# Counting sparse-graph edges by pairs of nodes: shared slots for every pair, and 512 instead of 496 counted chunks

## The chip, the cores and the metric

The kernel runs on one core of one Trainium2 chip. The time is the device time of one launch in microseconds (us), the median of several executions. The engines named below are PE (TensorE: matmuls), PEld (its weight loads), DVE (VectorE), ACT (ScalarE), POOL (GpSimd, which issues the indirect gathers) and SP (SyncE, which issues the plain transfers).

## The reference

A graph layer: 12,500 nodes with 128 features, 200,000 edges sorted by destination, four edge types. The destinations are drawn as 12500 times the square of a uniform number, so that nodes with low numbers have very many edges (several hundred for the first ones) and nodes with high numbers have some eight.

```python
h = jnp.maximum(_layernorm(x, axis=-1), 0.0)
xs = h[src]
msgs = 0
for i in range(4):
    msgs = msgs + where(edge_type == i, xs @ W[i] + b[i], 0.0)
out = x + segment_sum(msgs, dst, num_segments=12500)
```

## The kernel before

Edges are cut into 1563 chunks of 128. The first C0 = 496 chunks (the edges of the low-numbered, crowded nodes) are **counted**; the other TM = 1067 chunks are **gathered**.

**Gathered chunks.** They go in groups of G = 16. For each chunk POOL issues one indirect DMA that fetches the 128 source rows (`gather`, line 450, issue at line 456). The first RAW = 8 groups fetch rows of x and normalize them on the way (the raw stage), because the table of normalized rows, `htab`, is being built in that time; later groups fetch rows of `htab`, each in three bf16 parts. `sum_up` (line 469) makes one-hot matrices on DVE (line 479), multiplies rows by them on PE (line 517; three matmuls for a chunk), copies the sums to SBUF on ACT (line 524), multiplies by W on PE (line 534) and adds the result into a ring of nodes on DVE (line 546). The gathered rows lie in five buffers of eight chunks, so POOL can be up to forty chunks ahead of PE.

**Counted chunks.** For a counted node nothing is gathered. The kernel makes the matrix "how many edges of type t come from source node s" and multiplies the whole table by it. Sources are split into a block number (NW = 98 blocks) and a place in it (128). `make_slots` (line 676) sorts the edges of the counted nodes into **slots**, columns of 128 edges that belong to one node or to a pair, and leaves for each slot two vectors: `loT` (place of the source) and `hkT` (block and type of the source, 1 to 392). It runs within the raw stage, a few steps in each group (SLOT_STEPS, line 68), and what is left at the end of group 7. `levels[k]` is how many nodes (or pairs) are given a (k+1)-th slot.

`count` (line 808) turns slots into counts: DVE makes two one-hot matrices for a slot, `o1` (128 edges by 128 places, lines 820 and 824) and `o2` (128 edges by 392, line 825); PE multiplies them (line 829) into a PSUM tile of 128 by 392; slots of the same **unit** are summed there; ACT writes the result as 16-bit integers and reads the sum out (line 832). A unit holds two nodes: edges of the first weigh 1, edges of the second 256, so that the two bytes of an integer are the counts of the two nodes, and are later read as two 8-bit floats. Below node PAIRS = 558 a node has slots of its own, and a unit sums up to two slots of the one node with weight 1 and up to two of the other with weight 256 (a fixed number in the instruction). From node 558 up two neighbours share one slot, and each edge has its own weight in `byT` (a second per-edge vector in the instruction, line 823).

`multiply` (line 853) takes a **batch** of up to VBMAX = 112 nodes (56 units): it streams the whole table from DRAM and multiplies each block's three parts by the counts (line 864): 98 x 3 = 294 matmuls with 112 x 4 = 448 columns each. One such round over the table is called a pass. Then come eight small matmuls by W (line 879) and additions into `acc`, the sums of the counted nodes (line 887).

**Order.** `dense_work` (line 909) runs the count of a batch beside the multiply of the batch before; the first batch is counted with no multiply beside it. `pace` (line 896) spreads this work evenly, by columns, over the gathered groups from group 8 to the last full one; what is left goes in there, and the last small groups (12, 8, 4 and 3 chunks) follow. With 496 chunks the planner's lines 103 to 166 give: ND = 1304 counted nodes, NS = 1496 slots made, NSLOTS = 1123 slots counted (neighbours share from 558 on) in 670 units, in 12 batches: one of 108 nodes, 11 of 112. The batches have 54, 137, 137, 112, 83 (seven times) and 102 slots. The gathered chunks make 65 full groups and the four small ones.

Of the kernel before, what the change touches and what calls it, by code (L numbers as in the profile page):

```python
# [48 lines left out]
P = 128  # L49
# [7 lines left out]
C0 = 496  # L57
VBMAX = 112
MANY = 16
HB = 4  # L60
# [11 lines left out]
def kernel(  # L72
# [31 lines left out]
    ND = int(N * q**2 + 5 * 2 * q * N * (q * (1 - q) / E) ** 0.5) // 8 * 8 + 8  # L104
    caps = []
    for d in range(ND):
        many = E * (((d + 1) / N) ** 0.5 - (d / N) ** 0.5)
        caps.append(max(1, -(-int(many + 6 * many**0.5) // P)))
# [8 lines left out]
    def window_of(c):  # L117
# [8 lines left out]
    PAIRS = next(  # L126
        d
        for d in range(levels[1] + levels[1] % 2, ND, 2)
        if (lambda m: m + 6 * m**0.5)(E * (((d + 2) / N) ** 0.5 - (d / N) ** 0.5)) <= P
    )  # L130
    alone = [(k, d) for k in range(0, len(levels), 2) for d in range(min(levels[k], PAIRS))]
    if len(alone) % 2:
        alone.append(None)
    shared = [(0, d) for d in range(PAIRS, ND)]

    VB = VBMAX
    left = len(alone) + len(shared)
    sizes_of = ([left % VB] if left % VB else []) + [VB] * (left // VB)
    batches = []
    a = b0 = 0  # L140
    for i, n in enumerate(sizes_of):

        na, ns = len(alone) - a, len(shared) - b0
        n1 = 0 if i < 1 else min(round(n * na / (na + ns) / 2) * 2, na)
        n1 = max(n1, n - ns)
        batches.append(alone[a : a + n1] + shared[b0 : b0 + n - n1])
        a, b0 = a + n1, b0 + n - n1
    assert a == len(alone) and b0 == len(shared)

    def slots_of(u):  # L150

        if u[0] is not None and u[0][0] == 0 and u[0][1] >= PAIRS:
            return [(u[0][1], None)]
        got = []
        for v, by in zip(u, (1.0, 256.0)):
            if v is not None:
                k, d = v
                got.append((starts_of[k] + d, by))
                if k + 1 < len(levels) and d < levels[k + 1]:
                    got.append((starts_of[k + 1] + d, by))  # L160
        return got

    def units(vs):
        return [tuple(vs[i : i + 2]) for i in range(0, len(vs), 2)]

    NSLOTS = sum(len(slots_of(u)) for vs in batches for u in units(vs))
# [138 lines left out]
    def prep_dense():  # L305
# [7 lines left out]
        nc.vector.tensor_single_scalar(first1, di[:, n, 0], 1.0, op=ALU.add)  # L313
# [4 lines left out]
        nc.vector.tensor_scalar(what[:, 0], di[:, n], 1.0, 2047.0, ALU.add, ALU.min)  # L318
# [8 lines left out]
        nc.vector.tensor_sub(what[:, 1], lo[:, n], over[:, n])  # L327
# [10 lines left out]
    nc.vector.tensor_copy(iota_b, iota_i)  # L338
    iota_f = prep.tile([P, P], F32, name="iota_f")
# [336 lines left out]
    def make_slots(dix):  # L676
# [4 lines left out]
        nth = dix.tile([P, ND], F16, name="nth")  # L681
        packed = dix.tile([P, NS], I32, name="packed")
        cnt12 = dix.tile([N3, NS], BF16, name="cnt12")
        for a in range(0, ND, NB):
            z = min(a + NB, ND)
            nc.vector.tensor_single_scalar(d1[:, a:z], iota_n[:, : z - a], float(a), op=ALU.add)
# [20 lines left out]
        yield from pipelined(first_chunk(a, z) for a, z in pieces(ND))  # L707
        d = 0
        while d < ND:
            e = d  # L710
            while e < ND and caps[e] == caps[d]:
                e += 1
            nc.vector.tensor_scalar(nth[:, d:e], d1[:, d:e], 0.0, float(caps[d]), ALU.mult, ALU.add)
            d = e
        nc.vector.tensor_add(nth, nth, qa[:, :ND])
# [6 lines left out]
        def pick_out(q, a, z, before):  # L722
# [20 lines left out]
            if before:  # L743
                nc.vector.tensor_mul(mask[:, :n], pv[:, :n], mask[:, :n])
                nc.vector.tensor_add(packed[:, a:z], packed[:, a:z], mask[:, :n])
            else:
                nc.vector.tensor_mul(packed[:, a:z], pv[:, :n], mask[:, :n])

        jobs = []
        for a, z in pieces(NS):  # L750
            jobs.append(pick_out(qa, a, z, False))
            if a < ND:
                jobs.append(pick_out(nth, a, min(z, ND), True))
        yield from pipelined(jobs)

        def unpack(a, z):
            n = z - a
            hk = dix.tile([P, 512], I32, name="hk")
            nc.vector.tensor_single_scalar(hk[:, :n], packed[:, a:z], 7, op=ALU.arith_shift_right)
            nc.vector.tensor_copy(hkT[:, a:z], hk[:, :n])  # L760
            nc.vector.scalar_tensor_tensor(
                loT[:, a:z], hkT[:, a:z], float(-P), packed[:, a:z], op0=ALU.mult, op1=ALU.add
            )

            nc.vector.tensor_single_scalar(hk[:, :n], hk[:, :n], NT - 1, op=ALU.bitwise_and)
            ohs = []
            for t in range(NT):
                is_t = dix.tile([P, 512], BF16, name="sel", bufs=2 * DENSE)
                if t < NT - 1:
                    nc.vector.tensor_single_scalar(is_t[:, :n], hk[:, :n], t + 1.0, op=ALU.is_equal)  # L770
                else:
                    nc.vector.tensor_single_scalar(is_t[:, :n], hkT[:, a:z], 0.5, op=ALU.is_gt)
                ohs.append(is_t)
            yield True
            pn = x_ps.tile([N3, 512], F32, name="pt")
            for t in range(NT):
                nc.tensor.matmul(pn[:, :n], pick_a[:, t, :], ohs[t][:, :n], start=(t == 0), stop=(t == NT - 1))
            nc.scalar.copy(cnt12[:, a:z], pn[:, :n])
# [4 lines left out]

        one, two = slice(PAIRS, ND, 2), slice(PAIRS + 1, ND, 2)
        nc.vector.tensor_scalar(byT, hkT[:, two], 0.5, 255.0, ALU.is_gt, ALU.mult)
        nc.vector.tensor_single_scalar(byT, byT, 1.0, op=ALU.add)
        for of in (loT, hkT):
            nc.vector.tensor_tensor(of[:, one], of[:, one], of[:, two], ALU.add)
        nc.vector.memset(seen, 0.0)
        nc.vector.tensor_reduce(seen[:N3], cnt12, AX.X, ALU.add)  # L790

        for a, z in pieces(ND):
            pn = x_ps.tile([P, 512], F32, name="pt")
            todo = [k for k, n in enumerate(levels) if n > a]
            for k in todo:
                n = min(levels[k], z) - a
                nc.tensor.matmul(
                    pn[:, :n],
                    b12,
                    cnt12[:, starts_of[k] + a : starts_of[k] + a + n],  # L800
                    start=(k == todo[0]),
                    stop=(k == todo[-1]),
                )
            yield True
            nc.vector.tensor_tensor(acc[:, a:z], acc[:, a:z], pn[:, : z - a], ALU.add)


    def count(vs, counts):
        todo = []
        for i, u in enumerate(units(vs)):  # L810
            of = slots_of(u)
            todo += [(i, c, by, n == 0, n == len(of) - 1) for n, (c, by) in enumerate(of)]
        both = sdp.tile([P, VB // 2], F32, name="both", bufs=2)
        for s0 in range(0, len(todo), OB):
# [3 lines left out]
            for k, (i, s, by, first, last) in enumerate(part):  # L818
                if by == 1.0:
                    nc.vector.tensor_scalar(o1[:, k, :], iota_b, loT[:, s : s + 1], None, ALU.is_equal)  # L820
                else:
                    if by is None:
                        by = byT[:, (s - PAIRS) // 2 : (s - PAIRS) // 2 + 1]
                    nc.vector.tensor_scalar(o1[:, k, :], iota_b, loT[:, s : s + 1], by, ALU.is_equal, ALU.mult)  # L824
                nc.vector.tensor_scalar(o2[:, k, :], iota_n, hkT[:, s : s + 1], None, ALU.is_equal)  # L825
            for k, (i, s, by, first, last) in enumerate(part):
# [12 lines left out]
        n = len(vs) // 2  # L839
# [13 lines left out]
    def multiply(vs, counts):  # L853
        nv = len(vs)
# [26 lines left out]
        while i < nv:  # L881
            if vs[i] is None:
                i += 1
                continue
            k, d = vs[i]
            n = next((m for m in range(1, nv - i) if vs[i + m] != (k, d + m)), nv - i)
            nc.vector.tensor_tensor(acc[:, d : d + n], acc[:, d : d + n], py[:, i : i + n], ALU.add)
            i += n
# [17 lines left out]
    def dense_columns():  # L906
        return NSLOTS * float(NB) + sum(len(vs) for vs in batches) * NW * 3.0 * NT

    def dense_work():
# [5 lines left out]
        total = dense_columns() + sum(len(slots_of(u)) for u in units(batches[0])) * (alone_slot - a_slot)  # L915
        gone = 0.0
        before = None
        for vs in batches + [None]:
            steps = {}
            now = None  # L920
            if vs:
                now = vs, dense.tile([P, NW, VB // 2 * NT], U16, name="counts")
                steps[count(*now)] = sum(len(slots_of(u)) for u in units(vs)) * (a_slot if before else alone_slot)
            if before:
                steps[multiply(*before)] = len(before[0]) * a_node
# [21 lines left out]
    byT = slots.tile([P, (ND - PAIRS) // 2], F32, name="byT")  # L947
# [268 lines left out]
```

## Time and profile before

| | |
|---|---|
| median of 12 runs | 1398.63 us (1395.96 to 1399.77) |
| the profiled execution's own time, and its span | 1400.13 us, 1398.4 us |
| mean granted TensorE clock | 0.951 |
| busy: PE, DVE, ACT, POOL | 1277.6, 990.1, 600.5, 1041.8 us |
| multiply matmuls (line 864) | 3528, 736.2 us |
| count matmuls (line 829) | 1123, 271.5 us |
| gathers (line 456) | 128 of x, 939 of the table; 128.9 and 911.3 us |
| evictions of counts (line 832) | 670, mean 504 ns, and 670 reads of the sum, mean 211 ns |

The profile is of one execution. Busy times of an engine are sums of its instructions' times without double counting within the engine; a group's mean duration includes pipelining, so that the distance between starts of two neighbours is often shorter than the mean. A line of the table of groups reads: source line, engine, operation, output and inputs, shapes, number, busy time and mean, and then how long the engine had been idle before these instructions and what ended that.

### The profile page before, as it was taken

To read this page: it belongs to the slowest core of one execution; us is meant where nothing else is said; L and a number is where in the kernel's file an instruction comes from. 1 tells how busy PE (TensorE), PEld (TensorE's weight loads), DVE (VectorE), ACT (ScalarE), POOL (GpSimd) and SP (SyncE) were. 2 spreads that over 40 slices of the span, in tenths; PEclk is the share of its full clock that TensorE was granted. 3 is DMA by queue.
4 is the path that set the end of the run, shared out by engine and by line. 5 is a ranking of instruction groups with operands and counts; after the bars stand their busy time and mean duration, and the time that the engine had idled before them with its cause. 6 is when DMAs were issued, how large, how long until landed. Compare 5 with 4: busy or idle time off the path is not lost.

```text
span 1398.4 us, 28832 instructions
## 1 busy us (share of the span) xinstructions
PE 1277.6 (91%) x8981; PEld 764.3 (55%) x8981; DVE 990.1 (71%) x5329; ACT 600.5 (43%) x1993; POOL 1041.8 (74%) x1077
## 2 busy tenths in 40 slices
PE   1655887899999999999989999999999999999995
PEld 1434554455655555565545555555555555555563
DVE  8778897888888767675756675768766767775334
ACT  6766746335325245353443443534434335334111
POOL 7777757777777777777777777777777777777774
PEclk9985667899999999999999999999999999999997
DMA  6552333565665666666657666666666666666663
GB/s 166 188 153 95 137 108 88 149 189 181 200 181 174 196 192 201 193 203 192 206 156 209 185 205 193 192 198 197 195 194 191 194 194 189 187 188 186 212 193 97
DMA packets 129448, 249.81 MB, mean 179 GB/s; under 512 B 25255, under 2 KB 72025, under 8 KB 129289
## 3 DMA queue, kind: packets, MB, share of 16 engines
q1 hardware_dynamic: 80121, 147.17, 33.9%
q0 software_dynamic: 49168, 100.76, 24.9%
q8 instruction: 71, 1.16, 0.3%
q14 instruction: 88, 0.72, 0.1%
HBM read 231.80 MB, written 16.03 MB: 177 GB/s over the span
## 4 chain that ended last, share of the span: by engine, by line
PE 80%; DVE 11%; ACT 5%; issue 2%; DMA 0%; POOL 0%; DVEq 0%; SPq 0%; ACTq 0%
PE pa L864 46%; PE pt L829 13%; PE py L534 9%; PE ps L517 8%; ACT h L408 2%; DVE st L389 2%; ACT counts L832 2%; DVE ring L546 2%; PE ps L502 1%; DVE h L428 1%; PE py L879 1%; DVE oh L479 1%; DVE ohf L479 1%; DVE o L824 1%; PE pt L576 1%
## 5 line engine op out<-in xcount | busy, mean ns | idle before, releaser
L456 POOL DMA_INDIRECT hm<-htab,srcT x939 | 911.3, 971 | 300.0 <-issue 262.8
L864 PE MATMUL pa<-counts,hs 128*128 128x448 fp8e4 (+1 forms) x3528 | 736.2, 353 | 1.0 <-ACT counts L832 0.9
L864 PEld LDWEIGHTS <-hs 128*128 128x128 bf16 x3528 | 343.6, 98 | 306.9 <-issue 15.0
L832 ACT ACTIVATE counts<-pt 128x392 uint16<-128x392 f32 x670 | 328.1, 504 | 254.4 <-PE pt L829 251.9
L825 DVE TENSOR_SCALAR o<-iota_n,hkT 128x392 bf16<-128x392 f16 x1123 | 374.7, 334 | 0.0
L829 PE MATMUL pt<-o,o 128*128 128x392 bf16 x1123 | 271.5, 334 | 5.3 <-ACT counts L832 3.1
L546 DVE TENSOR_TENSOR ring<-ring,py 128x20 f32 (+7 forms) x1040 | 177.9, 171 | 92.7 <-PE py L534 70.3
L524 ACT COPY sb<-ps 128x224 f32<-128x224 f32 (+8 forms) x267 | 103.1, 394 | 255.8 <-PE ps L517 220.2
L479 DVE TENSOR_SCALAR oh<-iota_b,keyT 128x56 bf16<-128x56 bf16 (+7 forms) x939 | 163.3, 262 | 57.1 <-PE ps L517 55.5
L820 DVE TENSOR_SCALAR o<-iota_b,loT 128x128 bf16<-128x128 bf16 x375 | 100.0, 267 | 113.2 <-PE pt L829 106.1
L824 DVE TENSOR_SCALAR o<-iota_b,loT,byT 128x128 bf16<-128x128 bf16 x373 | 126.2, 338 | 58.2 <-PE pt L829 55.5
L456 POOL DMA_INDIRECT hm<-in_x_dram,srcT x128 | 128.9, 1007 | 40.7 <-issue 36.0
L534 PE MATMUL py<-sb,wsb 128*128 128x224 f32 (+7 forms) x520 | 146.7, 427 | 0.7 <-ACT sb L524 0.5
L517 PEld LDWEIGHTS <-hm 128*128 128x128 bf16 x2817 | 122.0, 99 | 45.2 <-DMA hm<-htab,srcT 6.7
L517 PE MATMUL ps<-oh,hm 128*128 128x56 bf16 (+7 forms) x2817 | 137.3, 198 | 5.3 <-DMA hm<-htab,srcT 5.0
L832 ACT ACTIVATION_READ_ACCUMULATOR counts<-pt 128x1 f32 x670 | 141.1, 211 | 0.0
L829 PEld LDWEIGHTS <-o 128*128 128x128 bf16 x1123 | 101.4, 99 | 71.7 <-DVE o L825 7.7
L534 PEld LDWEIGHTS py<-sb,wsb 128*128 128x128 f32 x520 | 101.3, 211 | 31.9 <-issue 7.5
L506 ACT CAST cnt<-ps 128x320 bf16<-128x320 f32 (+9 forms) x69 | 26.5, 384 | 207.3 <-PE ps L502 189.8
L517 PE MATMUL ps<-ohf,hm 128*128 128x40 f32 (+1 forms) x256 | 60.7, 400 | 58.7 <-ACT hm L408 58.6
L824 DVE TENSOR_SCALAR o<-iota_b,loT 128x128 bf16<-128x128 bf16 x375 | 98.2, 262 | 8.7 <-PE pt L829 8.5
L517 PEld LDWEIGHTS ps<-ohf,hm 128*128 128x128 f32 x256 | 54.7, 308 | 75.3 <-ACT hm L408 62.2
(188 smaller groups left out, 625.6 us busy)
## 6 DMA issues: line engine op xcount, KB each, us to landing
hs<-htab SPq DMA_DIRECT2D x288, 384.0 KB
hm<-htab,srcT POOLq DMA_INDIRECT x939
htab<-h SPq DMA_DIRECT2D x11, 768.0 KB
xo<-in_x_dram SPq DMA_DIRECT2D x23, 256.0 KB
out_dram<-xo SPq DMA_DIRECT2D x23, 256.0 KB
xt<-in_x_dram SPq DMA_DIRECT2D x6, 512.0 KB
hs<-htab SPq DMA_DIRECT2D x12, 192.0 KB
xt<-in_x_dram SPq DMA_DIRECT2D x5, 448.0 KB
```

The lines of the kernel that those rows point to most:

```text
L456: nc.gpsimd.indirect_dma_start(out=rows[:, (i - h0) * width : (i - h0 + 1) * width], out_offset=None, in_=table, in_offset=bass.IndirectOf ...
L479: nc.vector.tensor_scalar(oh[:, i, :], (iota_f if raw else iota_b)[:, :K], keyf[:, (t0 + i) % (TURN * P) : (t0 + i) % (TURN * P) + 1], Non ...
L517: mm = nc.tensor.matmul(ps[:, i - i0, :], rows(i, c, nparts), oh[:, i, :], start=(c == 0), stop=(c == nparts - 1),)
L524: nc.scalar.copy(sb[:, i0:i1].rearrange("p g t n -> p g (t n)"), ps[:, : i1 - i0, :])
L534: mm = nc.tensor.matmul(py[:, :g, :], wsb[:, t, :], sb[:, :g, t, :], start=False, stop=(t == NT - 1))
L546: nc.vector.tensor_tensor(to, to, py[:, i, :], ALU.add)
L820: nc.vector.tensor_scalar(o1[:, k, :], iota_b, loT[:, s : s + 1], None, ALU.is_equal)
L824: nc.vector.tensor_scalar(o1[:, k, :], iota_b, loT[:, s : s + 1], by, ALU.is_equal, ALU.mult)
L825: nc.vector.tensor_scalar(o2[:, k, :], iota_n, hkT[:, s : s + 1], None, ALU.is_equal)
L829: nc.tensor.matmul(pb, o1[:, k, :], o2[:, k, :], start=first, stop=last)
L832: nc.scalar.activation(counts[:, :, i * NT : (i + 1) * NT], pb.rearrange("p (b t) -> p b t", t=NT), AF.Copy, accum_out=both[:, i : i + 1],)
L864: nc.tensor.matmul(pa[:, : nv * NT], hs[:, j - j0, c * D : (c + 1) * D], counts[:, j, : nv * NT], start=(j == 0 and c == 0), stop=(j == NW ...
```

## The change

Two things are changed together.

First, the form of the slots. All counted nodes are taken as pairs of neighbours (2u, 2u+1); U = ND / 2 pairs. The edges of a pair share slots from the first one on, each edge carries its weight (1 or 256) in `byT`, and a unit is one pair, which sums up to SL = 4 slots. A pair with more than four slots has several units. `o1` is now always made with two per-edge vectors. To keep the parity of the destination, its bit is carried in the packed number (doubled place of the source, plus the bit), so `prep_dense` has more operations, and `unpack` takes the bit out, makes `byT` for all slots and counts edges by type twice (all edges, and those of odd nodes). `iota_2` holds even numbers to compare with the doubled places.

Second, C0 goes from 496 to 512: 512 chunks are counted and 1051 are gathered. With it the same planner lines give ND = 1392, NS = NSLOTS = 1080 slots in 711 units, in 13 batches: one of 39 units (78 nodes) and 12 of 56 (112 nodes); 39, 124, 104, 83 and then 79 or 80 slots for each, 93 in the last. The gathered chunks make 64 full groups and the same four small ones.

```diff
-C0 = 496
+C0 = 512
+SL = 4
...
+    U = ND // 2
     caps = []
-    for d in range(ND):
-        many = E * (((d + 1) / N) ** 0.5 - (d / N) ** 0.5)
+    for u in range(U):
+        many = E * (((2 * u + 2) / N) ** 0.5 - (2 * u / N) ** 0.5)
         caps.append(max(1, -(-int(many + 6 * many**0.5) // P)))
...
+    both_of = [(k, u) for k in range(0, len(levels), SL) for u in range(levels[k])]
+    double = [(k, u) for k, u in both_of if k + 1 < len(levels) and u < levels[k + 1]]
+    single = [v for v in both_of if v not in double]
     VB = VBMAX
-    left = len(alone) + len(shared)
+    left = len(both_of)
-    sizes_of = ([left % VB] if left % VB else []) + [VB] * (left // VB)
+    sizes_of = ([left % (VB // 2)] if left % (VB // 2) else []) + [VB // 2] * (left // (VB // 2))
...
+    def slots_of(v):
+        k, u = v
+        return [starts_of[m] + u for m in range(k, min(k + SL, len(levels))) if u < levels[m]]
...
+        nc.vector.tensor_single_scalar(pair[:, n], di[:, n], 1, op=ALU.arith_shift_right)
+        nc.vector.tensor_single_scalar(first1, pair[:, n, 0], 1.0, op=ALU.add)
...
+        nc.vector.tensor_single_scalar(di[:, n], di[:, n], 1, op=ALU.bitwise_and)
...
+        nc.vector.tensor_sub(bo[:, n], lo[:, n], over[:, n])
+        nc.vector.scalar_tensor_tensor(what[:, 1], di[:, n], 0.5, bo[:, n], op0=ALU.mult, op1=ALU.add)
...
+            nc.vector.tensor_single_scalar(par[:, :n], packed[:, a:z], 1, op=ALU.bitwise_and)
...
+            nc.vector.tensor_sub(loT[:, a:z], loT[:, a:z], par[:, :n])
+            nc.vector.tensor_scalar(byT[:, a:z], par[:, :n], 255.0, 1.0, ALU.mult, ALU.add)
...
+            for second in (False, True):
+                if second:
+                    nc.vector.scalar_tensor_tensor(
+                        hk[:, :n], par[:, :n], float(NT), hk[:, :n], op0=ALU.mult, op1=ALU.add
+                    )
...
+        nc.vector.tensor_sub(cnt12, cnt12, cnt2)
...
-            for k, (i, s, by, first, last) in enumerate(part):
-                if by == 1.0:
-                    nc.vector.tensor_scalar(o1[:, k, :], iota_b, loT[:, s : s + 1], None, ALU.is_equal)
-                else:
-                    if by is None:
-                        by = byT[:, (s - PAIRS) // 2 : (s - PAIRS) // 2 + 1]
-                    nc.vector.tensor_scalar(o1[:, k, :], iota_b, loT[:, s : s + 1], by, ALU.is_equal, ALU.mult)
+            for k, (i, s, first, last) in enumerate(part):
+                nc.vector.tensor_scalar(
+                    o1[:, k, :], iota_2, loT[:, s : s + 1], byT[:, s : s + 1], ALU.is_equal, ALU.mult
+                )
...
     def multiply(vs, counts):
-        nv = len(vs)
+        nv = 2 * len(vs)
```

## The prediction

> **What bounds the kernel now.** First the page's busy shares and slices, to see where each engine is full.
>
> ```profile
> PE 1277.6 (91%) x8981; PEld 764.3 (55%) x8981; DVE 990.1 (71%) x5329; ACT 600.5 (43%) x1993; POOL 1041.8 (74%) x1077
> ...
> PE   1655887899999999999989999999999999999995
> ...
> DVE  8778897888888767675756675768766767775334
> ...
> POOL 7777757777777777777777777777777777777774
> PEclk9985667899999999999999999999999999999997
> ```
>
> PE is full from the eighth slice on. POOL is level at seven tenths from beginning to end, which looks like slack and is not, as its timeline shows:
>
> ```profile
> 1379.70 0.95 POOL L456 DMA_INDIRECT hm<-htab,srcT  x1 [0.31 <-issue]
> 1380.95 0.95 POOL L456 DMA_INDIRECT hm<-htab,srcT  x1 [0.30 <-issue]
> 1382.21 0.95 POOL L456 DMA_INDIRECT hm<-htab,srcT  x1 [0.30 <-issue]
> ```
>
> A gather starts every 1.254 us, and the idle 0.30 us is "issue", no wait for a buffer. This spacing holds all through: 1067 x 1.254 = 1338 us, the last at 1382. So two engines are near their limits: POOL needs 16 x 1.254 = 20.07 us for a group, and PE must fit a group's share of counted work into the same time. Whether PE does is read from the busy times in five stages (raw groups, their second half, the first batch's count alone, the main stage, the tail); columns: length, PE, PEld, DVE, ACT, POOL, granted clock, DMA share, GB/s.
>
> ```profile
> 0.00:120.00 120.00, 57.77 (x212) 42.29 (x213) 98.35 (x547) 81.54 (x195) 90.24 (x100) 0.91 0.55 165
> 120.00:217.00 97.00, 73.79 (x319) 48.32 (x318) 81.02 (x386) 55.57 (x140) 64.60 (x62) 0.66 0.33 110
> 217.00:252.00 35.00, 26.64 (x164) 13.33 (x163) 29.44 (x149) 28.89 (x117) 26.46 (x29) 0.74 0.27 77
> 252.00:1357.00 1105.00, 1092.79 (x8060) 641.58 (x8059) 762.95 (x4154) 427.51 (x1526) 840.54 (x868) 0.99 0.64 191
> 1357.00:1399.00 42.00, 26.62 (x233) 18.80 (x232) 18.37 (x98) 7.03 (x16) 19.91 (x21) 0.83 0.44 125
> ```
>
> The main stage leaves PE 1105 - 1092.8 = 12.2 us idle, at clock 0.99. A busy PE need not be at its peak, so the last view is the PE timeline inside it:
>
> ```profile
> 696.08 2.43 PE L864 MATMUL pa<-counts,hs 128*128 128x448 fp8e4 x12
> 698.35 0.66 PE L829 MATMUL pt<-o,o 128*128 128x392 bf16 x3
> 698.85 0.42 PE L517 MATMUL ps<-oh,hm 128*128 128x64 bf16 x9
> ...
> 699.60 2.43 PE L864 MATMUL pa<-counts,hs 128*128 128x448 fp8e4 x12
> 701.87 0.66 PE L829 MATMUL pt<-o,o 128*128 128x392 bf16 x3
> 702.37 2.43 PE L864 MATMUL pa<-counts,hs 128*128 128x448 fp8e4 x12
> 704.64 0.27 PE L532 MATMUL py<-cnt,b 128*128 128x256 bf16 x1
> ```
>
> By distances of starts, 12 multiply matmuls take 698.35 - 696.08 = 2.27 us, 0.189 us each, and three of a count 0.50, 0.166 each. 448 / 0.189 and 392 / 0.166 are both 2.37 columns a ns: time goes with columns, back to back. In the main stage every column added on PE is time added.
>
> **The passes.** Before: 11 passes of 448 columns and one of 432. After: 12 of 448 and one of 78 x 4 = 312. With 0.189 us for 448, by columns 0.182 for 432 and 0.132 for 312, the difference is 294 x (0.189 + 0.132 - 0.182) = **+40.9 us**. If the short matmuls took as long as the full ones it would be 294 x 0.196 = +57.6; two rows lie on one line through zero, so I take columns. The lower end is 294 x (0.189 + 0.098 - 0.182) = +31, with 0.098 us for a weight load of the same line if columns cost less than that. The eight small matmuls by W of a pass took 0.9 us (726.06 to 726.95): **+0.9**.
>
> Here a rule can be weighed. The Trainium skill's "TensorE: Matmul & The Clock Gate", section "Back-to-back issue gap", gives N / 2.4 + 2.5 ns for isolated matmuls, but says that in a stream of weight loads and matmuls N = 512 sustains some 131 ns. For 448 columns the first is 189.2 ns, which the timeline agrees with; the second, scaled to 448 columns (115 ns), would make the extra pass cost an estimated 25 us, and the trace, a stream of just that kind, does not show it.
>
> **The slots in the main stage.** Before, 1123 - 54 = 1069 slots; after, 1080 - 39 = 1041. On PE -28 x 0.166 = **-4.6 us**.
>
> **The gathered group.** 16 chunks fewer: one group of window 12 less on PE (the raw stage keeps eight groups). 48 matmuls at 0.04 us (12 in about 0.5), 0.3 for its counts by type, 0.1 for the bias, and the multiply by W: 256 columns took 706.48 - 704.75 = 1.73 us, so 192 take 1.3. Sum **-3.7 us**. POOL loses 16 x 1.254 = 20.1 us; as PE is full, this is no gain by itself.
>
> **The first batch alone.** In 217 to 252 PE waits 0.15 us after each count, for ACT or DVE:
>
> ```profile
> 244.70 0.33 PE L829 MATMUL pt<-o,o 128*128 128x392 bf16 x1 [0.15 <-ACT counts L832]
> 245.18 0.33 PE L829 MATMUL pt<-o,o 128*128 128x392 bf16 x1 [0.15 <-ACT counts L832]
> 245.66 0.33 PE L829 MATMUL pt<-o,o 128*128 128x392 bf16 x1 [0.15 <-ACT counts L832]
> ```
>
> A slot costs 0.48 us here, so 15 fewer are -7.2 us; if the whole stage scales, 35 x 15 / 54 = -9.7; if only PE's own time counted, -5. I take **-7.2**, the measured distance. The pacing puts 54 x 2.5 x 392 extra columns into its total before and 39 x 2.5 x 392 after, so about 2.0 groups lie in this stage before and 1.4 after; 0.6 of a group moves to the main stage: **+2.3**.
>
> **The slot making, in the raw stage.** On PE the selecting matmuls lose 608 + 1024 columns times 4 and 8 or so, the counting by type gains: in all some 12,000 columns fewer, at the 1.1 to 1.9 columns a ns that these ran at (clock 0.66) about -8 us. On DVE first-chunk search and selecting save about 8 us, but `unpack` has 14 operations on a piece instead of seven (each 0.41 to 0.67 us for 512): 3 x 3.6 = 10.4 us become 2.1 x 7.3 = 15.4; with the removed pair additions (-2), the new subtraction, more levels and `prep_dense`, DVE comes out within 1 us of before. The order shifts: more steps (25 instead of 23, by my count of the generator's yields) are left over for the end of group 7, where nothing hides them. ACT, DVE and PE take turns on the chain in this stage, so PE's saving counts in part: **-3**, ends -8 (all of it) and +5 (the longer `unpack` alone on the path).
>
> **The second batch.** Its count (124 slots) runs beside the short pass. DVE needs 0.22 + 0.23 us for a slot with two vectors (start to start; 0.16 + 0.23 without): 124 x 0.45 = 56, plus 3.8 groups at some 5.3 us and 4 us of small work, 80 us. PE has 38.8 + 124 x 0.166 + 3.8 groups x 4.7 = 77. So DVE ends last by a little, and whatever waits for `o2` in PE's order waits too: **+3**, ends 0 (DVE was at 82.05 of 95 us beside 137 slots in before's third batch, and PE had no gap) and +12 (gaps as at 700 to 740, where DVE, PE and gathers waited for each other, 5.7 us idle and the clock down to 0.86). In other batches DVE needs 80 x 0.45 + 4.5 x 5.3 + 4 = 64 of about 91 us: hidden by PE. ACT has 41 evictions more, about 0.47 us start to start, hidden by its idle half.
>
> **What no longer waits.** A group will need 20.5 us of PE against POOL's 20.07, so gathers stay ahead and the waits at 700 to 740 should shrink: **-4**, ends 0 and -8. In the tail PE is idle for 42 - 26.6 = 15.4 us, some of it behind the last gathers, which end about 20 us earlier against a dense end that comes later: **-2**, ends 0 and -8. The rest of the tail is the ring additions and output, unchanged.
>
> **Sum.** 40.9 + 0.9 - 4.6 - 3.7 - 7.2 + 2.3 - 3 + 3 - 4 - 2 = **+22.6 us** on the profiled execution's 1400.13. That execution is 1.5 us above the median, so I predict 1398.6 + 22.6 = 1421 us.
>
> **Rivals.** *Gathers bound it.* If the pass finds room on PE and POOL sets the end, 16 gathers fewer give 1398.6 - 20.1 = 1379. For it: POOL's unbroken spacing to 1382. Against it: PE would need 41 us of idle time in the main stage and has 12.2. It decides from the point where PE work for a group falls under 20.07 us; I find 20.5. *The savings are at their far ends*: -9.7, -8, -8, -8, no cost in the second batch: about +5, 1404. For it: raw stage and tail have PE idle in plenty. Against: they would all have to come. *DVE becomes the bound.* All 1080 `o1` take the 338 ns form, some 0.06 us longer by starts than the 750 that had a fixed weight or none. With bursts of DVE work in the batches of 124 and 104 slots and PE's clock falling with each gap, +10 to +25 more, about 1440. Against: average use stays near 70%. *It doesn't do what it says* (fewer than 13 batches, or the check of the slots failing): the sizes follow from constants, 711 / 56 = 12.7.
>
> **How the numbers follow.** About 0.2% (2.8 us) is what a measurement of this kernel tells from no change. Forecast (1410 to 1432) 0.72; DVE rival (1432 to 1450) 0.12; savings at their ends (1400 to 1410) 0.10, a fifth of it within 0.2%; gathers bound 0.05; the rest 0.01. Leaving out the gathers' case, the lower part of the savings' and the upper of DVE's, the range is 1405 to 1435, and the likeliest case's own is 1410 to 1432. Faster 0.05, same 0.03, slower 0.92.
>
> **What would show it.** Multiply matmuls 3822, about 189 ns apart; 711 evictions; 1051 gathers; the first count alone some 7 us shorter; PE full between it and the last pass, and POOL now waiting for PE's buffers (a gap other than 0.30 us) before the end. Wrong would be: PE idle of over 20 us in the main stage (DVE), an end that follows the last gather by 15 us as now (gathers bound), or the raw stage ending more than 8 us off 217.

## The result, and the profile after

| | before | after |
|---|---|---|
| median | 1398.57 us (28 runs, 1395.96 to 1400.39) | 1418.7 us (7 runs, 1417.4 to 1423.58) |
| ratio, 95% interval | | 1.0154 [1.0145, 1.0164] |
| profiled execution: own time, span | 1400.13, 1398.4 us | 1417.24, 1415.4 us |

The kernel is slower by 20.1 us by the medians; 1421 had been forecast. The runs of after lie in two clumps, four at 1417.4 to 1418.7 and three at 1422.1 to 1423.6, for a reason that was not found, and the profiled execution is in the lower one, so that the two traces differ by 17.0 us only; what is said below of stages is set against those 17.0.

Busy shares and slices, from the page of after:

```profile
PE 1299.3 (92%) x9205; PEld 785.9 (56%) x9205; DVE 1005.6 (71%) x5244; ACT 620.2 (44%) x2074; POOL 1021.4 (72%) x1061
...
PE   1647888889999999999999999999999999999995
...
DVE  8787888887876776766767667687677666776324
...
POOL 7777667777767777777777777776777767777762
PEclk9986557999999999999999999999999999999999
```

PE has 21.7 us more to do, POOL 20.4 us less. POOL's last slice fell from 4 to 2: the last gather is issued 24.2 us ahead of the end, instead of 16.2. How the gathers are issued is seen in POOL's timeline and its waits of after:

```profile
670.30 0.95 POOL L450 DMA_INDIRECT hm<-htab,srcT  x1 [0.31 <-issue]
...
674.43 0.97 POOL L450 DMA_INDIRECT hm<-htab,srcT  x1 [3.19 <-PE pt L835]
...
1391.20 0.95 POOL L450 DMA_INDIRECT hm<-htab,srcT  x1 [0.30 <-issue]
```

```profile
POOL hm L450 <- PE pt L835: 45.7, 49, 3.2
POOL hm L450 <- PE ps L511: 9.8, 10, 3.1
```

(A line of waits reads: who waits, for whom; us in all, times, longest.) These are 59 waits for PE, 55.5 us together. 25 of them are no longer than the steady 0.30 us of issue, and before has such ones too; the other 34 last 0.4 to 3.2 us, 47.8 us together, and before has none of these: POOL is so far ahead that no buffer is free. This is the turn of the bound that was forecast. 1051 gathers need 1318 us at 1.254 us; PE no longer lets them go at that speed.

For the readings by stage I cut both traces at the same four events: the first count alone, the first multiply matmul, the end of the first pass, and the end of the last pass. Columns as before: length, PE, PEld, DVE, ACT, POOL, clock, DMA share, GB/s. First the kernel before, cut in this new way, then after:

```profile
0.00:216.73 216.73, 131.29 (x528) 90.49 (x529) 179.10 (x930) 137.09 (x334) 154.57 (x161) 0.80 0.46 141
216.73:252.31 35.58, 27.21 (x170) 13.70 (x168) 29.79 (x151) 28.90 (x118) 27.04 (x29) 0.74 0.28 79
252.31:350.20 97.89, 93.78 (x724) 54.90 (x723) 82.56 (x456) 35.71 (x132) 74.72 (x77) 0.95 0.60 180
350.20:1356.10 1005.90, 997.80 (x7337) 585.88 (x7333) 679.90 (x3697) 391.26 (x1396) 764.76 (x792) 1.00 0.64 192
1356.10:1399.00 42.90, 27.52 (x239) 19.35 (x236) 18.79 (x98) 7.57 (x17) 20.66 (x22) 0.83 0.44 124
```

```profile
0.00:217.26 217.26, 131.71 (x554) 92.11 (x555) 178.44 (x955) 138.11 (x337) 158.88 (x165) 0.78 0.46 142
217.26:241.56 24.30, 18.73 (x147) 9.47 (x144) 22.85 (x123) 21.25 (x89) 18.69 (x19) 0.74 0.28 79
241.56:323.30 81.74, 73.21 (x601) 50.45 (x602) 72.18 (x354) 32.56 (x124) 62.36 (x64) 0.94 0.67 201
323.30:1376.80 1053.50, 1051.30 (x7674) 615.76 (x7673) 714.01 (x3718) 420.68 (x1513) 769.78 (x803) 1.00 0.65 194
1376.80:1416.00 39.20, 24.39 (x238) 18.08 (x236) 18.14 (x97) 7.58 (x17) 11.69 (x13) 0.93 0.39 112
```

| stage | before | after | difference |
|---|---|---|---|
| raw groups and slot making | 216.7 | 217.3 | +0.5 |
| first count alone | 35.6 | 24.3 | -11.3 |
| first pass, beside the second batch's count | 97.9 | 81.7 | -16.2 |
| the other passes | 1005.9 | 1053.5 | +47.6 |
| tail, to the span's end | 42.3 | 38.6 | -3.7 |

The main stage (rows three and four) grew by 31.4 us: PE's busy time by 32.9, its idle time from 12.2 to 10.7. So it is work on PE, not waiting, that made the kernel slower. Inside, the idle time has moved: beside the first pass it rose from 4.1 to 8.5, in the rest it fell from 8.1 to 2.2, with PE busy 99.8% of 1053 us. Waits for gathered rows are gone from PE's matmuls on them, as their lines on the pages of before and after show (the last numbers are PE's idle time just ahead of them):

```profile
L517 PE MATMUL ps<-oh,hm 128*128 128x56 bf16 (+7 forms) x2817 | 137.3, 198 | 5.3 <-DMA hm<-htab,srcT 5.0
```

```profile
L511 PE MATMUL ps<-oh,hm 128*128 128x56 bf16 (+7 forms) x2769 | 136.2, 198 | 0.0
```

That a short pass is priced by its columns is seen in PE's timeline of after:

```profile
241.56 1.75 PE L870 MATMUL pa<-counts,hs 128*128 128x312 fp8e4 x12
243.15 0.33 PE L835 MATMUL pt<-o,o 128*128 128x392 bf16 x1
```

12 matmuls of 312 columns take 1.59 us from start to start, 0.1325 us each; 0.132 had been forecast from the 448-column ones. The figure for isolated matmuls in the Trainium skill ("TensorE: Matmul & The Clock Gate", section "Back-to-back issue gap") puts 312 columns at an estimated 132.5 ns, and the timeline agrees.

### The profile page after: what moved, and what is told of

Same layout as the page of the kernel before. It is cut to its first block, busy times and chain, and to the rows that moved or that the text cites. A ratio compares the mean times of both kernels' runs of the same rounds, so it can differ in the third digit from the quotient of the medians.

```text
span 1415.4 us, 29284 instructions
## 1 busy us (share of the span) xinstructions
PE 1299.3 (92%) x9205; PEld 785.9 (56%) x9205; DVE 1005.6 (71%) x5244; ACT 620.2 (44%) x2074; POOL 1021.4 (72%) x1061
## 3 DMA queue, kind: packets, MB, share of 16 engines
q1 hardware_dynamic: 83659, 156.80, 35.3%
q0 software_dynamic: 48400, 99.19, 24.7%
## 4 chain that ended last, share of the span: by engine, by line
PE 80%; DVE 12%; ACT 4%; issue 2%; DMA 1%; DVEq 1%; SPq 0%; ACTq 0%
PE pa L870 48%; PE pt L835 12%; PE ps L511 8%; PE py L528 8%; DVE st L383 2%; ACT h L402 2%; DVE ring L540 2%; DVE oh L473 1%; PE ps L496 1%; PE py L885 1%; DVE o L828 1%; DVE ohf L473 1%; DVE h L422 1%; ACT counts L838 1%; DVE o L831 1%
## 5 line engine op out<-in xcount | busy, mean ns | idle before, releaser
L450 POOL DMA_INDIRECT hm<-htab,srcT x923 | 889.9, 964 | 329.4 <-issue 265.6
L870 PE MATMUL pa<-counts,hs 128*128 128x448 fp8e4 (+1 forms) x3822 | 779.6, 349 | 0.7 <-issue 0.5
L870 PEld LDWEIGHTS <-hs 128*128 128x128 bf16 x3822 | 372.8, 98 | 323.1 <-issue 10.6
L828 DVE TENSOR_SCALAR o<-iota,loT,byT 128x128 bf16<-128x128 bf16 x1080 | 361.7, 335 | 193.2 <-PE pt L835 187.1
L838 ACT ACTIVATE counts<-pt 128x392 uint16<-128x392 f32 x711 | 348.0, 504 | 210.9 <-PE pt L835 209.7
L831 DVE TENSOR_SCALAR o<-iota_n,hkT 128x392 bf16<-128x392 f16 x1080 | 353.2, 327 | 0.0
L518 ACT COPY sb<-ps 128x192 f32<-128x192 f32 (+8 forms) x263 | 101.9, 392 | 295.5 <-PE ps L511 279.3
L473 DVE TENSOR_SCALAR oh<-iota_b,keyT 128x56 bf16<-128x56 bf16 (+7 forms) x923 | 159.9, 260 | 62.6 <-PE ps L511 62.3
L500 ACT CAST cnt<-ps 128x224 bf16<-128x224 f32 (+10 forms) x68 | 26.2, 385 | 210.9 <-PE ps L496 189.2
L511 PE MATMUL ps<-ohf,hm 128*128 128x40 f32 (+1 forms) x256 | 64.1, 413 | 55.1 <-ACT hm L402 55.1
L402 ACT ACTIVATE hm<-hm,nmr,rstd 128x128 f32<-128x128 f32 x128 | 51.0, 481 | 8.8 <-DVE nmr L393 8.3
L402 ACT ACTIVATE h<-xt,nmrt,rstdt 128x128 f32<-128x128 f32 x98 | 39.3, 483 | 0.0
```

The lines of the kernel that those rows point to most:

```text
L402: nc.scalar.activation(h(k), xt(k), AF.Relu, bias=nmr[:r, k : k + 1], scale=rstd[:r, k : k + 1])
L450: nc.gpsimd.indirect_dma_start(out=rows[:, (i - h0) * width : (i - h0 + 1) * width], out_offset=None, in_=table, in_offset=bass.IndirectOf ...
L473: nc.vector.tensor_scalar(oh[:, i, :], (iota_f if raw else iota_b)[:, :K], keyf[:, (t0 + i) % (TURN * P) : (t0 + i) % (TURN * P) + 1], Non ...
L511: mm = nc.tensor.matmul(ps[:, i - i0, :], rows(i, c, nparts), oh[:, i, :], start=(c == 0), stop=(c == nparts - 1),)
L518: nc.scalar.copy(sb[:, i0:i1].rearrange("p g t n -> p g (t n)"), ps[:, : i1 - i0, :])
L828: nc.vector.tensor_scalar(o1[:, k, :], iota_2, loT[:, s : s + 1], byT[:, s : s + 1], ALU.is_equal, ALU.mult)
```

## The experiments

Two theories stood against each other at first. Mine: PE is full, the 13th pass is paid in full, and the new slots are a gain that is too small to pay for it. The rivals: gathers set the end, or DVE (all `o1` with two vectors, batches of 124 and 104 slots) does.

### e1: the new slots with the old 496 chunks

```diff
-C0 = 512
+C0 = 496
```

> The new slots with 496 counted chunks, so that only the form of the slots differs from before (1036 slots instead of 1123, 667 units instead of 670, still 12 passes; 51, 128, 107, then 82 slots in a batch). PE theory with a gather floor: PE loses (1069 - 985) x 0.166 = 13.9 us of counts and 294 x 0.010 = 3.0 us in the first pass, but the 1067 gathers still need 1338 us and the last is issued near 1382, 15 us before the end; so the time stays at 1394 to 1398 and PE shows 10 us or more of new idle time, with waits for gathered rows. PE alone (no floor): 1381. DVE rival (two per-edge vectors in every o1 are dear): 1400 or more.

Measured: 1391.26 us, ratio to before 0.9949 [0.9937, 0.9962]. This is some 3 us under the range with the gathers' floor, and 10 over what PE alone would give. So the two halves of the change have opposite signs: the slots gain 7.3 us, and going on from 496 to 512 chunks costs 27.4. The last three stages of e1 show why the gain is not larger:

```profile
254.04:345.80 91.76, 87.51 (x696) 53.22 (x697) 80.30 (x425) 35.43 (x131) 69.81 (x73) 0.98 0.66 188
345.80:1330.60 984.80, 982.96 (x7281) 578.49 (x7278) 681.64 (x3563) 389.81 (x1397) 747.64 (x779) 1.00 0.68 195
1330.60:1391.00 60.40, 35.30 (x238) 23.11 (x236) 18.41 (x97) 7.61 (x17) 35.08 (x37) 0.74 0.41 112
```

The main stage is 27.2 us shorter than before's (1076.6 against 1103.8), but the tail is 60.0 to the span's end instead of 42.3. Its timeline on PE, PE's waits for gathered rows in all, and the last gather on POOL:

```profile
1334.45 0.30 PE L511 MATMUL ps<-oh,hm 128*128 128x96 bf16 x3 [0.95 <-DMA hm<-htab,srcT]
1337.03 0.42 PE L511 MATMUL ps<-oh,hm 128*128 128x96 bf16 x3 [2.27 <-DMA hm<-htab,srcT]
...
1369.65 0.33 PE L511 MATMUL ps<-oh,hm 128*128 128x104 bf16 x3 [0.99 <-DMA hm<-htab,srcT]
```

```profile
PE ps L511 <- DMA hm<-htab,srcT: 10.0, 11, 2.3
```

```profile
1375.71 0.95 POOL L450 DMA_INDIRECT hm<-htab,srcT  x1 [0.30 <-issue]
```

PE is done with the passes at 1330.6 and then waits for gathered rows; the last gather is issued 45 us later, and the kernel ends 14.9 us after it. At 496 chunks the gathers are the bound, and they eat 18 of the 27 us: 10.0 as waits, and 7.8 because PE is busy longer in this tail than in before's (35.3 us for 238 matmuls against 27.5 for 239), at a granted clock of 0.74 against 0.83.

### e5 and e10: 496 chunks, gathers started earlier

POOL's waits in e1 name one that can be shortened without a change to the count:

```profile
POOL hm L450 <- DMA htab<-h: 11.5, 1, 11.5
```

It waits 11.5 us for the table of normalized rows. With one more group gathered from x it has work in that time.

```diff
-C0 = 512
+C0 = 496
...
-RAW = 8
+RAW = 9
```

> The new slots with 496 counted chunks and nine raw groups instead of eight. With eight, gathers end last (the last at 1375.7, 15 us before the end; PE is through with the passes at 1331) and POOL stands 11.5 us waiting for the table of rows. A ninth raw group gathers from x in that time. Gather theory: up to 11 us earlier, 1380 to 1386, with PE's passes some 20 us later, since the counted work starts a group later. If PE needs the time that the ninth raw group takes from it (raw groups keep PE half idle), 1390 to 1400.

Measured: 1388.9 us, 0.9936 [0.9922, 0.995], just above the range of the gather theory. The last gather went out at 1365.10 instead of 1375.71, 10.6 us earlier, as the gather theory has it; the span got only 4.1 shorter, because the passes, after a longer raw stage (238.7 instead of 221.6), now end at 1345.9 and the tail begins there. The end of the passes and the last gather had been 45 us apart and are now 19, and in this tail (40.6 us) PE has no wait for gathered rows any more. e10 adds the even dealing of slots that e9 (below) tests:

> The version with 496 counted chunks and nine raw groups, with the crowded pairs dealt out evenly (88 slots in the second batch instead of 128). There PE idles 4.7 us in the first pass's stage; passes end 41 us and gathers 21 us before the end, so PE bounds it a little: 1 to 4 us faster than without, 1385 to 1388, if DVE is the cause of that idle time; 1389 if not, or if the tail's gathers take it back.

Measured: 1385.68 us, 0.991 [0.9893, 0.9926], the fastest kernel of the study, faster than before and than after (by 33 us). Its first-pass stage and its tail:

```profile
271.03:348.80 77.77, 77.44 (x616) 46.88 (x615) 61.61 (x329) 34.40 (x129) 59.00 (x62) 0.99 0.70 206
...
1341.20:1384.00 42.80, 27.44 (x238) 19.24 (x236) 18.29 (x98) 7.57 (x17) 20.02 (x22) 0.83 0.44 122
```

The first pass beside the second batch's count leaves PE 0.3 us idle (4.7 in e5). The end follows the last gather (1366.68) by 16.3 us, but the gathers do not set it: in this tail, too, PE has no wait for gathered rows, and the tail is 41.8 us long, near before's 42.3.

### e6 and e7: what a column costs in each pass

Both are the kernel after with one part of three left out of one pass: e6 of the seventh batch's, a full one; e7 of the first batch's, the short one.

```diff
+        parts = 2 if vs is batches[6] else 3
...
-                for c in range(3):
+                for c in range(parts):
...
-                        stop=(j == NW - 1 and c == 2),
+                        stop=(j == NW - 1 and c == parts - 1),
```

(e7 has `batches[0]`.)

> As the changed kernel, but one full pass in the middle (the seventh batch) multiplies two of the three bf16 parts of the table: 98 matmuls of 448 columns are left out (and the smallest part of the rows for its 112 nodes). Column theory: 98 x 0.189 = 18.5 us faster, 1400, still over the gathers' floor of about 1378. If matmuls were hidden behind DVE or gathers, 0 to 5 us.

> As the changed kernel, but the short first pass (312 columns) multiplies two of the three parts: 98 matmuls left out. Column theory: 98 x 0.1325 = 13.0 us faster, 1406. If DVE bounds the second batch's count beside it, only the sparse work that moves there gains: 0 to 5 us, 1414 to 1419.

Measured: e6 1401.61 us, 1.0026 [1.0016, 1.0035], 17.1 less than after; e7 1420.82, 1.0167 [1.0151, 1.0184], no gain at all (1414 to 1419 had been given for the case in which DVE is the bound). In e6's row of the other passes the whole saving is seen:

```profile
324.70:1359.30 1034.60, 1033.03 (x7576) 606.20 (x7575) 708.69 (x3718) 420.05 (x1513) 766.44 (x801) 1.00 0.69 197
```

1053.5 has become 1034.6: 98 matmuls less, 18.9 us less, 0.193 each (0.174 by the medians; 0.189 is the distance of starts). A full pass's columns are paid in full. In the short pass they are not. e7's first-pass stage, and its gaps on PE:

```profile
241.94:322.00 80.06, 64.30 (x503) 41.86 (x504) 71.77 (x354) 32.57 (x123) 61.26 (x62) 0.89 0.69 207
```

```profile
258.90 0.27 PE L496 MATMUL ps<-oh,three 128*32 128x192 bf16 x4 [3.99 <-DVE oh L473]
...
282.07 0.35 PE L496 MATMUL ps<-oh,three 128*32 128x192 bf16 x4 [5.02 <-DVE oh L473]
...
306.05 0.35 PE L496 MATMUL ps<-oh,three 128*32 128x192 bf16 x4 [5.17 <-DVE oh L473]
```

98 matmuls of 0.1325 us, 13.0 us, are left out; PE's busy time fell by 8.9 us only, at a granted clock of 0.89 instead of 0.94, and the stage is 1.7 us shorter. (In the profiled execution the tail, 41.6 us against 38.6, takes this back; tails are compared further down.) PE waits instead for `oh` (the one-hot matrices of a gathered group, line 473), which stands on DVE behind the `o1` and `o2` of the second batch: ahead of the gap at 282, DVE's timeline of e7 has nothing but these from 271.8 to 277.9, and the first `oh` at 278.04. After has two such gaps, of 4.14 and 4.17 us, at 260.8 and 306.7; e7 has three, two of them longer. Here DVE sets the length.

### e3 and e9: the load on DVE beside the short pass

e3 makes every `o1` without the weight, as the cheaper instruction with one vector:

```diff
-                    o1[:, k, :], iota_2, loT[:, s : s + 1], byT[:, s : s + 1], ALU.is_equal, ALU.mult
+                    o1[:, k, :], iota_2, loT[:, s : s + 1], None, ALU.is_equal
```

> As the changed kernel, but o1 is made with one per-edge vector, the weight of 256 for odd nodes is left out (so the counts of a pair are all put on its even node). DVE saves 0.06 us on each of 1080 slots, 65 us in all. PE bound: at most 4 us faster, from the short-pass stage (242 to 323), the only stage of the main part in which PE idles: 1415 to 1419. DVE bound: 10 us faster or more, below 1409.

Measured: 1413.19 us, 1.0117 [1.0102, 1.0132], 5.5 less than after, just below what the PE theory allowed and far from what DVE as the bound of the whole would give. The two stages of e3 say where:

```profile
243.37:317.50 74.13, 70.49 (x599) 48.70 (x600) 65.55 (x352) 32.52 (x123) 56.76 (x58) 1.00 0.74 220
317.50:1371.10 1053.60, 1051.97 (x7675) 615.51 (x7673) 672.43 (x3718) 420.79 (x1514) 777.55 (x807) 1.00 0.67 194
```

DVE has 41.6 us less to do in the other passes, and their time is the same to 0.1 us. Beside the short pass DVE has 6.6 less, and the stage is 7.6 shorter.

e9 keeps the instruction and changes who is in the second batch. The pairs with over two slots, which after puts first, are dealt evenly over the 12 full batches; the second batch then has 85 slots instead of 124, and the other full ones 83 to 90.

```diff
+    heavy = [v for v in double if v[0] + 2 < len(levels) and v[1] < levels[v[0] + 2]]
+    light = [v for v in double if v not in heavy]
+    part = lambda vs, i: vs[len(vs) * i // 12 : len(vs) * (i + 1) // 12]
+    double = [v for i in (5, 4, 3, 2, 1, 0, 6, 7, 8, 9, 10, 11) for v in part(heavy, i) + part(light, i)]
```

> As the changed kernel, with the crowded pairs dealt out evenly over the batches: 85 slots in the second batch (beside the short pass) instead of 124, 85 to 90 in the others; the same columns in all. If DVE makes PE idle in the short pass's stage (8.5 us now, and none gained there when a third of its matmuls was left out), that idle time falls to 3 us or less and the kernel is 4 to 6 us faster: 1413 to 1415. If the idle time there has another cause (the one-hots of the gathered groups being queued behind, whatever the number of slots), 0 to 2 us.

Measured: 1411.27 us, 1.0095 [1.0078, 1.0112], 7.4 less than after, where 4 to 6 had been expected.

```profile
242.31:304.90 62.59, 61.77 (x553) 44.75 (x552) 51.74 (x266) 32.87 (x125) 47.76 (x49) 1.00 0.78 234
304.90:1368.70 1063.80, 1060.17 (x7731) 620.23 (x7729) 735.42 (x3828) 419.61 (x1513) 782.08 (x815) 1.00 0.68 194
```

The short pass's stage is 19.2 us shorter and PE is idle 0.8 us in it instead of 8.5; the other passes take 10.3 more, since the 39 slots (39 x 0.166 = 6.5 us of PE) and a part of the gathered groups are now there. The rival of DVE as the bound was right for one pass out of thirteen, and worth some 7 us there. The table's transfers from DRAM, which a shorter pass needs faster, are no rival for this stage: in e9 it lasts 62.6 us at a DMA share of 0.78, with PE idle 0.8 us.

### e8: one count by type

`unpack` counts edges by type twice, all of them and those of odd nodes. e8 leaves the second count out:

```diff
+        nc.vector.memset(cnt2, 0.0)
...
-            for second in (False, True):
+            for second in (False,):
```

> As the changed kernel, but unpack counts edges by type once instead of twice (the separate count of odd nodes is left out, so the bias of a pair goes to its even node). Takes away 5 DVE operations, 4 matmuls and one copy on each piece: DVE 2.1 x 2.4 = 5 us in the raw stage. If unpack lies on the path at the raw stage's end, the first count starts 3 to 5 us earlier and the time falls by as much; if it is hidden behind normalizing and the raw groups, 0 to 1 us.

Measured: 1414.55 us, 1.0115 [1.0099, 1.0131], 4.1 less than after. The raw stage:

```profile
0.00:212.87 212.87, 128.61 (x542) 92.16 (x543) 175.31 (x941) 136.45 (x334) 153.89 (x163) 0.77 0.48 144
```

It ends 4.4 us earlier, with 3.1 us less of DVE work and 3.1 less of PE work in it. This count lies on the path, whole. The last pass, too, ends 4.3 us earlier (1372.5); in the profiled execution the tail (41.8 us against after's 38.6) takes 3.2 of it back, so that e8's gain is read from these stages rather than from the 4.1 us of the medians.

### e2 and e4: more than four slots to a unit

e2 lets a unit sum up all the slots of its pair, so that no pair needs a second unit. e4 did the same with 504 chunks and crowded pairs dealt over the batches.

```diff
-SL = 4
+SL = 24
```

> As the changed kernel, with up to 24 slots summed in a unit instead of four: 696 units instead of 711, and all 15 come off the short first batch (24 units; its pass has 192 columns instead of 312; batches of 24, 162, 102, 84 slots). Column theory alone: the pass falls by 294 x (0.132 - 0.098) = 10 us (its weight loads, 0.098 us, are the floor), the count of the first batch alone by 15 x 0.62 = 9 us, 2.5 us come back in the main stage: 1402. If DVE bounds the second batch (162 slots x 0.45 us = 73 us, plus some 21 us for its groups, against 71 us of PE), about 16 us come back there as idle PE: 1417 to 1420.

> The new slots with 504 counted chunks, up to 24 slots in a unit, and the crowded pairs spread over the batches: 672 units, just 12 full passes, batches of 56, 98, 92, 91, 87, 105 and about 85 slots, 1059 gathers. If the balance of PE columns and gathers sets the time: against before, PE has +2 us of passes, -11 of counts, -2 of gathered chunks; gathers end 8 x 1.254 = 10 us earlier; so 1386 to 1391, faster than both kernels. If the slots' form costs what the columns don't show (DVE, evictions), 1395 to 1402.

Measured: 26199 and 26154 us. The trace of e2 has a group of 3126 matmuls that is in no other trace:

```profile
L1150 PE MATMUL pm<-wsb,ht 128*128 128x512 f32 x3126 | 3243.8, 1141 | 599.6 <-DVE ht L1148 599.6
```

It belongs to the slow loop at the kernel's end, which computes everything anew when one of the kernel's own guards trips. By the code, the guard that depends on the slots of a unit is `most > MANY`: within a unit, no node may get more than 16 edges whose sources have the same place (one of 128, whatever the block). Counted over the edges that the reference draws with its default seed, the most is 12 with four slots to a unit, and 25 with 24 slots, for 512 as for 504 chunks: node 0 has 1784 edges, and they no longer lie in several units. So this guard trips in e2 and e4; a run with another limit was not made. The time as such says nothing, but the part ahead of the slow loop can be read, at the same events:

```profile
232.32:328.80 96.48, 77.22 (x631) 50.97 (x632) 88.22 (x430) 31.68 (x121) 62.34 (x63) 0.87 0.59 172
328.80:1385.00 1056.20, 1053.19 (x7715) 617.82 (x7714) 711.26 (x3710) 422.64 (x1521) 779.55 (x811) 1.00 0.67 194
```

The pass's columns got fewer (192 a matmul instead of 312), and the stage is 14.7 us longer: the second batch now has 162 slots, and PE idles 19.3 us. The first pass began 9 us earlier, and the last one ended some 8 us later than in after. Like e7 it shows that the short pass costs nothing by its columns while DVE's slots last longer. e4 gave no more than the guard.

One more reading from e2's timeline of PE:

```profile
232.32 1.15 PE L870 MATMUL pa<-counts,hs 128*128 128x192 fp8e4 x12 [0.35 <-issue]
233.31 0.49 PE L835 MATMUL pt<-o,o 128*128 128x392 bf16 x2
```

12 matmuls of 192 columns take 0.99 us, 0.0825 each. So the 0.098 us of a weight load, taken for a floor in the expectation of e2 and for the lower end of the passes' term in the prediction, is none: the price goes on falling with the columns.

## Why the prediction was right, step by step

The forecast of 1421 stands 2.3 us from the median, and the sum of +22.6 against 17.0 in the traces and 20.1 in the medians. What it was mainly about, a pass priced by its columns on a full PE, held. That the total came so near is in part luck: the raw stage was 3.5 us dearer than forecast, the other three stages together 9.2 us cheaper. The terms, by stage:

| stage | forecast | in the traces |
|---|---|---|
| raw, slot making | -3 | +0.5 |
| first count alone | -7.2 | -11.3 |
| main: passes, W, slots, group, the moved 0.6 group, second batch, waits | 40.9 + 0.9 - 4.6 - 3.7 + 2.3 + 3 - 4 = +34.8 | +31.4 |
| tail | -2 | -3.7 |

**The passes (+40.9), slots and the gathered group.** Right in mechanism and near in size. PE's busy time in the main stage rose by 32.9; the forecast's PE terms (40.9, 0.9, -4.6, -3.7, 2.3) make 35.8. That columns set the price is shown by the 0.1325 us of the short matmuls, by the 0.0825 in e2 and by e6.

But the steps "the passes" and "the second batch" are not independent, and my sum took them so. The 294 short matmuls (39.0 us) lie beside a count that DVE bounds; e7 took 13.0 us of them away and gained nothing. The sum came out because I had also worked out the stage as a whole, PE 77 and DVE 80 us, with DVE last by a little. Measured: 73.2 and 72.2 busy, 81.7 long.

**The second batch (+3).** The mechanism was right in the main: DVE ends last, though PE waits for `oh`, behind the slots' one-hots, and hardly for `o2` itself. The idle time beside the first pass grew by 4.4 us. What this batch's load on DVE costs in all is more: 7.4 us by e9, which deals it out, and 5.5 by e3, which makes it lighter. That was within my bound of +12, and before had something like it (4.1 us idle beside 137 slots).

**The first batch alone (-7.2) and the moved group (+2.3).** The 0.48 us a slot held: counts that wait for ACT or DVE still start 0.48 apart (227.37, 227.85 and 228.32 in after), and with 15 slots fewer PE's waits for ACT there fell from 15 to 8. The rest of the -11.3 is an omission in my accounting. A part of the second gathered group did move out of this stage: 16 multiplies by W (line 534) stand in before's stage and eight (line 528) in after's, with the four transposes of line 576 (0.9 us by starts) no longer there either. I added what moved to the main stage and didn't take it off where it came from. On PE alone a move is no cost, and the +2.3 shouldn't have been in the sum.

**The slot making (-3).** Wrong in size, and in sign by a little: the step that failed is the saving of 8 us on PE. PE's busy time in this stage did not fall (131.3 us before, 131.7 after). By its lines, the selecting matmuls take 8.6 us less (24.7 to 16.1), but the counting by type takes 3.8 more (5.0 to 8.8), and the raw groups' own matmuls, the same number, 4.5 more (60.7 to 64.1 for the largest of the three groups), at a granted clock of 0.78 instead of 0.80. The longer `unpack` had been bounded by +5 if it lay on the path alone; e8 shows that its second count does lie there, with 4.4 us. So all the rest that changed in this stage came to some -4 us net (4.4 less the measured +0.5), and the two nearly cancel; which part of the rest gave it was not tried. (By the code `unpack` has 16 operations on a piece where before's has eight, not 14 and seven; the difference of some 5 us stays.)

**What no longer waits (-4).** -5.9, in the forecast's direction and within its ends, and for its reason: PE's waits for gathered rows are gone, and POOL's waits for PE's buffers are the sign that had been named for it.

**The tail (-2).** -3.7, but not for the reason given. The last gathers did not hold up before's tail: there PE waits for the ring's additions on DVE (7.4 us) and for ACT (1.1), and never for gathered rows. The length of the tail goes with the granted clock instead. It is 38.6 us at 0.93 in after, but 40.3 at 0.90 in e6, 40.0 at 0.89 in e3, 40.9 at 0.86 in e9, and 41.6 and 41.8 at 0.82 in e7 and e8, all with the same code in the tail; before has 42.3 at 0.83. At before's clock little is left of the gain. Why the clock differs there from execution to execution was not found.

**The rivals.** "Gathers bound it" had asked for a group's work on PE to fall under 20.07 us. After it doesn't; in e1 PE ends its passes 45 us ahead of the last gather, and PE waits for gathered rows in the tail: the rival was wrong for this change, and right for its first half alone. "DVE becomes the bound" was right for the first pass and wrong for the other 1053 us (e3: 41.6 us of DVE work less, no time less).

Open: in e1 the raw stage ends at 221.6, 4.3 us later than in after, with the same code and fewer edges to sort. The traces show when: its raw groups are 0.8 us behind after's at 82 us and 4.3 behind at 167. Why, they don't show.

## What to carry to other kernels

Where two engines are each a few per cent from the bound, a change that moves work between them is priced by the one that gets it: 16 chunks were taken from POOL, which lost 20 us of work and gave nothing back, and PE, which had 12 us idle in its main stage, got 33 us more there. Take such a change apart by its halves before you judge it: here one half gained 7 us and the other lost 27, and the gaining half, with a ninth group gathered from x and the load dealt evenly, gave 13 us. And add up a stage as the longest of its engines, not as a sum of differences: leaving out 98 matmuls gave 0.17 to 0.19 us for each in one pass and nothing in another, because the batch counted beside that one kept PE waiting for DVE.

## What the runs showed of the hardware that was not expected

The granted clock fell with PE's gaps within one stage: 0.94 in after's first-pass stage (8.5 us idle), 0.89 in e7's (15.8 idle), 0.87 in e2's (19.3), 1.00 in e3's (3.6) and e9's (0.8). Waits on a full PE cost more than their length here. e3's stage is 7.6 us shorter than after's: 4.9 us are idle time, the other 2.7 are busy time, with 599 matmuls instead of 601. In e7's stage the busy time fell by 8.9 us where 13.0 us of matmuls were left out. And in e1's tail 238 matmuls kept PE busy 7.8 us longer at 0.74 than before's 239 did at 0.83. That the clock is the whole of it was not tried by itself.

The spacing of the gathers was 1.25 to 1.26 us in every timeline that was read, with the DMA engines at 0.39 as at 0.78 of their time; the longer gaps are, but for a few, waits for a buffer or for the table.
